# A graph network's edge weights: computed by TensorE in each layer from stored attributes, instead of stored and loaded

## The chip, the cores and the metric

The kernel runs on one core of a Trainium2 chip. The metric is the device time of one execution in microseconds (us), lower is better. A core has five engines that work through queues of their own and wait for each other by semaphores: PE (TensorE, matrix products into PSUM, with weight loads shown apart as PEld), DVE (VectorE), ACT (ScalarE), POOL (GpSimd) and SP (SyncE, which here only issues DMAs). Tiles lie in SBUF or in PSUM, and DRAM is reached by DMA.

## The reference

Three layers of a graph network with three relations, on N = 6250 nodes of D = 256 features and E = 100000 edges with 32 attributes each, then a residual and a layer norm:

```python
ew = edge_attr @ edge_w + edge_b
inv_cnt = [1.0 / jnp.maximum(jax.ops.segment_sum(m, dst, num_segments=n), 1.0) for m in rel_masks]
for l in range(N_LAYERS):
    residual = x
    msg = jax.nn.relu(x[src] * ew)
    out = jnp.zeros((n, D), dtype=x.dtype)
    for i in range(NUM_REL):
        h = jax.ops.segment_sum(msg * rel_masks[i][:, None], dst, num_segments=n)
        h = h * inv_cnt[i][:, None]
        out = out + h @ weights[l, i]
    out = out + x @ roots[l] + biases[l]
    x = residual + jax.nn.relu(out)
```

and at the end `_layernorm(x0 + x)`. The edge weights `ew` (E x 256) are the same in all layers. All is in float32. The edges come sorted by destination, and `dst` grows with the square of the edge's place, so that low nodes have many edges and high nodes few.

## The kernel before

A short first part looks at the edge lists and chooses a path; these inputs take `ordered_path`. Its unit is a *pair* of edge tiles, 2 x 128 edges; there are U = 391 pairs, and 49 node tiles of 128 nodes. One Python loop per layer, over `it`, writes out the order of every engine's queue by hand (a manual schedule), with each stage of a pair at a fixed distance from `it`:

- `gather` (L571 to L577, POOL), for the pair 8 steps ahead (AHEAD): two indirect DMAs fetch the 128 + 128 source rows of x into a tile xs (16 buffers).
- `weigh` (L612, DVE), 3 steps ahead: xs times the edge weights, in place; `bound` (L615, ACT): ReLU.
- `one_hot` (L619, DVE), 3 steps ahead: a 0/1 matrix per tile, 3 relations x 40 nodes (WIN) wide; its bfloat16 copy oh_b (L623, ACT) in layer 0 alone.
- `reduce` (L629, PE), at `it`: the products of messages and one-hots, 128 features x 120 columns, into a PSUM tile h_p. In layer 0 it counts edges too.
- `add` (L645, DVE), LAG steps behind: h_p is added to the accumulator acc in SBUF at a place read from the edge list. LAG is 1 in layer 0 and 3 in layers 1 and 2, with 2 and 5 buffers of h_p.
- Node tiles, when their edges are done (`starts`): `node_mul` (L673, PE, 12 products), `node_end` (L704 and L705, DVE), the store of the new rows to x_mid in DRAM (L707, SP), `clear` of acc (L690, ACT). The root term of each node tile (L650, L654, L658, L661) is made earlier, spread over the layer. The last layer adds the norm.

A layer's gathers read what the layer before stored in x_mid, all of it, so each layer starts when the last node tile of the one before is stored. `schedule` (L818) turns the pairs' order so that the first K = 60 pairs come last.

The edge weights before: in layer 0 only, `load_attrs` (L527, SP) loads attributes, `turn` (L589, PE) transposes two pairs of them, `keep_attrs` (L595, ACT) copies them to SBUF, `make_ew` (L602, PE) makes four products of 33 attribute rows (32 and a one for the bias) with edge_w into the PSUM tile ew_p (one buffer[...]), and `keep_ew` (L609, ACT) copies that into ew_s in SBUF. `store_ew` (L581, SP) keeps ew_s in DRAM as ew_all, 256 KB a pair. In layers 1 and 2 `load_ew` (L552, SP) loads it again, four pairs at a time. `weigh` reads ew_s in every layer.

Of the kernel before, what the change touches and what calls it, by code (L numbers as in the profile page):

```python
# [8 lines left out]
F32 = mybir.dt.float32  # L9
BF = mybir.dt.bfloat16  # L10
I32 = mybir.dt.int32
AF = mybir.ActivationFunctionType
ALU = mybir.AluOpType
AX = mybir.AxisListType
PSUM = bass.MemoryType.PSUM
# [13 lines left out]
def general_path(  # L29
# [24 lines left out]
    NP = NT * P  # L54
    K = R * NP
    HI = K // P
# [386 lines left out]
def ordered_path(ctx, tc, x, edge_attr, weights, roots, biases, edge_w, edge_b, out, src_i, seg, place_i, consts):  # L443
# [4 lines left out]
    nc = tc.nc  # L448
    P = 128
    N, D = x.shape  # L450
# [5 lines left out]
    U = T // 2  # L456
    A1 = A + 1
    DC = D // P
    UP = P // 2
    AR = UP + A1  # L460
    WK = R * WIN
    AHEAD = 8
    order, _, moved, least, most = schedule(N, E, 1)
    reach = []
    for u, (lo, hi) in enumerate(zip(least, most)):
# [7 lines left out]

    dram = ctx.enter_context(tc.tile_pool(name="dram_o", bufs=1, space=DRAM))

    ew_all = dram.tile([(U + 3) // 4, P, 8 * D], F32, name="ew_all")
    x_mid = [dram.tile([N, D], F32, name=f"x_mid{l}") for l in range(L - 1)]

    big = ctx.enter_context(tc.tile_pool(name="big", bufs=1))
# [27 lines left out]
    edge = ctx.enter_context(tc.tile_pool(name="edge", bufs=2))  # L507
# [1 line left out]
    o_pool = ctx.enter_context(tc.tile_pool(name="o_p", bufs=1, space=PSUM))  # L509
    r_pool = ctx.enter_context(tc.tile_pool(name="r_p", bufs=1, space=PSUM))  # L510


    groups = list(dict.fromkeys(u // 4 for u in order))

    def first_of(p, n):
        return p == 0 or order[p - 1] // n != order[p] // n

    def last_of(p, n):
        return p == U - 1 or order[p + 1] // n != order[p] // n
# [25 lines left out]
        nc.sync.dma_start(b_sb, biases[l:l + 1, :].to_broadcast([P, D]))  # L545
        return r_sb, b_sb

    def load_ew(l, g):
        ew = edge.tile([P, 4, 2, D], F32, name="ew_s", bufs=3)
        if l > 0:  # L550
            n = min(4, U - 4 * g)
            nc.sync.dma_start(ew[:, :n].rearrange("p k i d -> p (k i d)"), ew_all[g, :, :n * 2 * D])  # L552
        return ew

    def layer(l, r_sb, b_sb, ews, pools):
        h_pool = pools.enter_context(tc.tile_pool(name="h_p", bufs=2 if l == 0 else 5, space=PSUM))
        if l == 0:
            ew_pool = pools.enter_context(tc.tile_pool(name="ew_p", bufs=1, space=PSUM))
            t_pool = pools.enter_context(tc.tile_pool(name="turn_p", bufs=1, space=PSUM))

        LAG = 1 if l == 0 else 3
        starts = schedule(N, E, LAG)[1]
        moved = schedule(N, E, LAG)[2]
        x_rows = x if l == 0 else x_mid[l - 1]
        w_sb = wpool.tile([P, R * DC, D], F32, name="w_sb")
        CH = DC + 1 if l == 0 else DC
        xs, ew_ps, ats, ohs, h_ps, turns, o_ps, rs = {}, {}, {}, {}, {}, {}, {}, {}
        x0s, mvs, oh_bs, t_ss, places = {}, {}, {}, {}, []
        r_next, ews_next = (None, None), {}

        def gather(u):  # L571
            xs[u] = edge.tile([P, 2, D], F32, name="xs", bufs=16)
# [3 lines left out]
                    out=xs[u][:, i, :], out_offset=None, in_=x_rows[:, :],  # L576
                    in_offset=bass.IndirectOffsetOnAxis(ap=src_i[:, t:t + 1], axis=0))  # L577

        def store_ew(g):
            n = min(4, U - 4 * g)  # L580
            nc.sync.dma_start(ew_all[g, :, :n * 2 * D], ews[g][:, :n].rearrange("p k i d -> p (k i d)"))  # L581

        def pairs_of(q):
            return range(min(2, U - 2 * q))
# [6 lines left out]

        def keep_attrs(q):
            n = len(pairs_of(q))
            ats[q] = edge.tile([AR, 2, P], F32, name="at", bufs=1)
            nc.scalar.activation(ats[q][:, :n], turns[q][:AR, :n, :], AF.Copy)  # L595

        def make_ew(q):

            ew_ps[q] = ew_pool.tile([P, 2, 2, D], F32, name="ew_p")
            for k in pairs_of(q):  # L600
                for i in range(2):
                    nc.tensor.matmul(ew_ps[q][:, i, k, :], ats[q][i * UP:i * UP + A1, k, :],  # L602
                                     ew_sb[i * UP:i * UP + A1, :], start=True, stop=True)

        def keep_ew(q):
            if q // 2 not in ews:
                ews[q // 2] = load_ew(0, q // 2)
            for k in pairs_of(q):
                nc.scalar.activation(ews[q // 2][:, q % 2 * 2 + k], ew_ps[q][:, :, k, :], AF.Copy)  # L609

        def weigh(u):
            nc.vector.tensor_mul(xs[u], ews[u // 4][:, u % 4], xs[u])  # L612

        def bound(u):
            nc.scalar.activation(xs[u], xs[u], AF.Relu)  # L615
# [125 lines left out]
        for it in range(-9, max(starts) + 6):  # L741
            def pair(k):
                return order[it + k] if 0 <= it + k < U else None
            if pair(AHEAD) is not None:
                gather(pair(AHEAD))
            if l == 0 and pair(9) is not None and first_of(it + 9, 4):
                load_attrs(pair(9) // 4)
            if l > 0 and pair(AHEAD) is not None and pair(AHEAD) // 4 not in ews:
                ews[pair(AHEAD) // 4] = load_ew(l, pair(AHEAD) // 4)
            if l == 0 and it >= -4 and (it + 4) % 20 == 0 and (it + 4) // 20 * 6 < NT - 1:  # L750
                load_x((it + 4) // 20 * 6)
            if it == 10:
                nc.sync.dma_start(w_sb, weights[l].rearrange("r (c p) e -> p (r c) e", p=P))
            if l == L - 1 and it + 2 in root_at:
                load_x0(root_at[it + 2])
            if l < L - 1 and it == U - 10:
                r_next = load_root(l + 1)
            if l < L - 1 and U <= it < U + 2:
                ews_next[groups[it - U]] = load_ew(l + 1, groups[it - U])

            if pair(0) is not None:
                reduce(pair(0))
            if pair(3) is not None:
                weigh(pair(3))
                bound(pair(3))
            if pair(-LAG) is not None:
                add(pair(-LAG))
            if l == 0:

                for k, work in ((4, keep_ew), (5, make_ew), (6, keep_attrs), (7, turn)):  # L770
                    if pair(k) is not None and first_of(it + k, 2):
                        work(pair(k) // 2)
                if pair(3) is not None and last_of(it + 3, 4):
                    store_ew(pair(3) // 4)
            if it in root_at:
                root_turn(root_at[it])
            if it - 1 in root_at:
                root_turned(root_at[it - 1])
            if it - 2 in root_at:
                root_mul(root_at[it - 2])  # L780
            if it - 4 in root_at:
                root_keep(root_at[it - 4])
            if it == moved:
                move()
            if it - 2 == moved:
                clear(P)
            if it + 1 in node_at and slot_of(node_at[it + 1]) == 0:
                wrap()
            if it in node_at:
                node_mul(node_at[it], 0)  # L790
            if it - 1 in node_at:
                node_mul(node_at[it - 1], 1)
            if it - 3 in node_at:
                node_end(node_at[it - 3])
                clear(slot_of(node_at[it - 3]))
            if it - 4 in node_at and l == L - 1:
                norm(node_at[it - 4])
            if pair(3) is not None:
                one_hot(pair(3))
        return (*r_next, ews_next)  # L800

    with tc.manual_schedule():
        state = (*load_root(0), {})
# [4 lines left out]

WIN = 40
RING = 1024
ASIDE = RING + WIN
ROOTS = 16
PACK = 2048


def schedule(N, E, lag):  # L818

    P = 128
    U = -(-E // (2 * P))
    NT = -(-N // P)
    done = []
    for c in range(NT):
        edges = E * min(1.0, (P * (c + 1) / N) ** 0.5)
        done.append(U if c == NT - 1 else min(U, -(-int(edges) // (2 * P)) + 4))  # L830
    K = -(-done[0] // 4) * 4
    order = list(range(K, U)) + list(range(K - 1, -1, -1))
    moved = done[1] - K + lag
    starts = [0] * NT
    step = moved
    for c in range(2, NT):
        step = starts[c] = max(done[c] - K + lag + 1, step + 4)

    whole = U - int(0.55 * K)
    starts[1] = max(whole + lag, step + 4)  # L840
    starts[0] = max(U + lag - 1, starts[1] + 4)

    node = lambda e: int(N * min(1.0, max(0.0, e / E)) ** 2)
    least = [node(2 * P * u - 1024) for u in range(U)]
    most = [node(2 * P * u + 1024) for u in range(U)]


    for p, u in enumerate(order, lag):
        if u >= K:
            assert all(p <= starts[c] or least[u] >= P * (c + 1) for c in range(2, NT))  # L850
            assert p <= moved or least[u] >= 2 * P
            assert all(p < starts[c] or least[u] >= P * c for c in range(8, NT, 8))
            for b in range(RING // P + 1, (most[u] + WIN - 1) // P + 1):
                assert (moved + 2 if b - RING // P == 1 else starts[b - RING // P] + 3) < p
        else:
            assert most[u] <= 2 * P and (p <= starts[1] or most[u] + WIN <= P)
    return order, starts, moved, least, most
# [149 lines left out]
```

## Time and profile before

| | before |
|---|---|
| median of 3 runs | 3129.4 us (3127.76 to 3131.86) |
| profiled execution | 3133.5 us |
| its span, first to last instruction | 3131.7 us |
| granted PE clock, mean | 0.855 |
| first gather of layers 0, 1, 2 starts at | 38.3, 1082.1, 2104.1 us |
| last gather of layers 0, 1, 2 starts at | 1064.9, 2086.5, 3111.4 us |
| DMA packets | 668.14 MB, mean 213 GB/s |

The profile is one execution, taken on the chip. Its page has each engine's busy time and share of the span, and rows of digits for 40 equal slices of it (tenths of busy time; for PEclk tenths of the full TensorE clock that was granted). A group's row reads: line, engine, operation, out<-in, shape and count, busy time, mean ns of one, then the idle time of the engine just before and what ended most of it. "issue" is idle time in which the engine waited for nothing that the profile shows. [...] Some answers of the trace are finer: who waited for whom, busy times by stretches of time, and instructions in order of time.

### The profile page before, as it was taken

What the parts mean: (1) busy time and instruction counts of PE and PEld (TensorE: products, weight loads), DVE (VectorE), ACT (ScalarE), POOL (GpSimd) and SP (SyncE); (2) the same over time, 40 slices, a digit from 0 to 9 for tenths busy, and PEclk for the clock granted to TensorE, in tenths of its full rate; (3) what the DMA queues carried; (4) which work ended last, traced back from release to release, by engine and by line L of the source; (5) the groups of instructions that cost most, each with busy time, mean ns of one, the idle gap of its engine ahead of it and who ended that gap; (6) DMA issues with size and microseconds to landing.
All of it is one profiled execution on the core that took longest, in us unless ns stands there. A gap on an engine that the chain in (4) does not pass through costs nothing.

```text
span 3131.7 us, 50860 instructions
## 1 busy us (share of the span) xinstructions
PE 2429.6 (78%) x14938; PEld 2108.6 (67%) x14938; DVE 2003.2 (64%) x4664; ACT 1302.0 (42%) x2524; POOL 2354.9 (75%) x3118
## 2 busy tenths in 40 slices
PE   4898999999998766677777777767677777877765
PEld 3777777778887666666666666656566666666665
DVE  4566666777776455566666666645566677777765
ACT  3666666666776422222333333222223333333332
POOL 7777777777777677777777777767777777777775
PEclk9899899999998778778888888766887888888886
DMA  4777776766776665656666666656666666666664
GB/s 135 233 233 231 222 241 213 228 216 217 230 231 213 217 218 199 213 200 218 205 217 205 221 221 217 206 184 223 211 208 223 220 217 209 224 228 216 218 216 138
DMA packets 295322, 668.14 MB, mean 213 GB/s; under 512 B 147224, under 2 KB 181996, under 8 KB 257788
## 3 DMA queue, kind: packets, MB, share of 16 engines
q1 hardware_dynamic: 175832, 350.27, 32.2%
q0 software_dynamic: 112608, 307.65, 31.6%
q10 hardware_dynamic: 6596, 6.87, 0.6%
q8 instruction: 124, 2.03, 0.3%
q14 instruction: 162, 1.33, 0.1%
HBM read 542.90 MB, written 121.70 MB: 212 GB/s over the span
## 4 chain that ended last, share of the span: by engine, by line
PE 31%; DMA 21%; issue 19%; POOL 17%; DVE 9%; ACT 2%; DVEq 1%; POOLq 0%; ACTq 0%
POOL xs L575 16%; PE h_p L629 15%; DMA xs<-x_mid,src_io 15%; PE o_p L673 7%; DMA xs<-in_x_dram,src_io 6%; PE ew_p L602 4%; DVE x_root L704 3%; DVE xs L612 2%; PE r_p L658 2%; DVE acc L645 2%; PE turn_p L589 1%; ACT ew_s L609 1%; POOL limits L926 1%; DVEq L645 1%; DVE oh L619 1%
## 5 line engine op out<-in xcount | busy, mean ns | idle before, releaser
L575 POOL DMA_INDIRECT xs<-x_mid,src_io x1564 | 1537.5, 983 | 509.0 <-issue 404.6
L629 PE MATMUL h_p<-oh,xs 128*128 128x120 f32 x9384 | 1451.6, 311 | 445.0 <-issue 177.8
L629 PEld LDWEIGHTS h_p<-oh,xs 128*128 128x128 f32 x9384 | 1364.3, 223 | 541.6 <-issue 309.4
L612 DVE TENSOR_TENSOR xs<-ew_s,xs 128x512 f32<-128x512 f32 x1173 | 808.0, 689 | 913.5 <-DMA xs<-x_mid,src_io 566.8
L615 ACT ACTIVATE xs<-xs 128x512 f32<-128x512 f32 x1173 | 739.5, 630 | 1484.9 <-DVE xs L612 1466.3
L575 POOL DMA_INDIRECT xs<-in_x_dram,src_io x782 | 789.6, 1010 | 247.1 <-issue 158.7
L645 DVE TENSOR_TENSOR acc<-h_p,acc 128x240 f32 (+1 forms) x1173 | 519.5, 443 | 147.0 <-PE h_p L629 74.7
L673 PE MATMUL o_p<-w_sb,acc 128*128 128x256 f32 (+1 forms) x1764 | 503.5, 428 | 89.2 <-DVE acc L645 52.1
L619 DVE TENSOR_TENSOR oh<-iota_w,seg_o 128x240 f32<-128x240 f32 x1173 | 467.0, 398 | 0.0
L673 PEld LDWEIGHTS o_p<-w_sb,acc 128*128 128x128 f32 (+1 forms) x1764 | 361.7, 216 | 152.4 <-DVE acc L645 57.6
L658 PE MATMUL r_p<-r_sb,t_s 128*128 128x256 f32 x588 | 216.3, 504 | 79.5 <-ACT t_s L654 78.8
L602 PE MATMUL ew_p<-ew_sb,at 33*128 33x256 f32 x1564 | 235.2, 421 | 10.9 <-ACT at L595 8.8
L609 ACT ACTIVATE ew_s<-ew_p 128x512 f32<-128x512 f32 x391 | 209.4, 587 | 41.5 <-PE ew_p L602 40.5
L704 DVE SCALAR_TENSOR_TENSOR x_root<-o_p,inv,x_root 128x256 f32<-128x256 f32 (+1 forms) x441 | 212.4, 482 | 20.9 <-PE o_p L673 8.6
L623 ACT ACTIVATE oh_b<-oh 128x240 bf16<-128x240 f32 x391 | 160.0, 409 | 117.9 <-DVE oh L619 111.0
L658 PEld LDWEIGHTS r_p<-r_sb,t_s 128*128 128x128 f32 x588 | 130.0, 245 | 111.3 <-ACT t_s L654 95.5
L602 PEld LDWEIGHTS ew_p<-ew_sb,at 33*128 33x128 f32 x1564 | 141.7, 195 | 44.8 <-ACT at L595 16.3
L690 ACT ACTIVATE acc<-zero_o 128x768 f32<-128x768 f32 (+1 forms) x150 | 141.0, 940 | 15.8 <-PE o_p L673 9.2
L629 PE MATMUL h_p<-oh_b,full_ones 128*128 128x120 bf16 x782 | 109.3, 223 | 0.0
L589 PE MATMUL turn_p<-ident_o,an 128*128 128x128 f32 x391 | 89.4, 312 | 7.9 <-DMA an<-in_edge_attr_dram 7.8
L589 PEld LDWEIGHTS turn_p<-ident_o,an 128*128 128x128 f32 x391 | 40.7, 145 | 77.1 <-issue 75.9
L650 PE MATMUL r_p<-ident_o,x_all 128*128 128x128 f32 x294 | 64.1, 303 | 30.9 <-DVE x_root L661 24.8
(84 smaller groups left out, 609.0 us busy)
## 6 DMA issues: line engine op xcount, KB each, us to landing
ew_s<-ew_all SPq DMA_DIRECT2D x194, 1024.0 KB
ew_all<-ew_s SPq DMA_DIRECT2D x97, 1024.0 KB
xs<-x_mid,src_io POOLq DMA_INDIRECT x1564
xs<-in_x_dram,src_io POOLq DMA_INDIRECT x782
an<-in_edge_attr_dram SPq DMA_DIRECT2D x97, 128.0 KB
x_mid<-x_all SPq DMA_DIRECT2D x96, 128.0 KB
x_all<-in_x_dram ACTq DMA_DIRECT2D x8, 768.0 KB
x<-in_x_dram SPq DMA_DIRECT2D x48, 128.0 KB
```

Of the source, the lines that this page charges most:

```text
L575: nc.gpsimd.indirect_dma_start(out=xs[u][:, i, :], out_offset=None, in_=x_rows[:, :], in_offset=bass.IndirectOffsetOnAxis(ap=src_i[:, t:t ...
L589: nc.tensor.transpose(turns[q][:, k, :], ans[groups.index(q // 2) % 3][:, q % 2 * 2 + k].rearrange("p i a -> p (i a)"), ident)
L602: nc.tensor.matmul(ew_ps[q][:, i, k, :], ats[q][i * UP:i * UP + A1, k, :], ew_sb[i * UP:i * UP + A1, :], start=True, stop=True)
L609: nc.scalar.activation(ews[q // 2][:, q % 2 * 2 + k], ew_ps[q][:, :, k, :], AF.Copy)
L612: nc.vector.tensor_mul(xs[u], ews[u // 4][:, u % 4], xs[u])
L615: nc.scalar.activation(xs[u], xs[u], AF.Relu)
L619: nc.vector.tensor_tensor(ohs[u], iota_w[:, None, :].to_broadcast([P, 2, WK]), seg[:, 2 * u:2 * u + 2, None].to_broadcast([P, 2, WK]), op= ...
L629: nc.tensor.matmul(h_ps[u][:, d, :], xs[u][:, i, d * P:(d + 1) * P] if d < DC else full_ones, (ohs if d < DC else oh_bs)[u][:, i, :], star ...
L645: nc.vector.tensor_tensor(there, h_ps[u][:, :CH].rearrange("p c (r w) -> p c r w", r=R), there, op=ALU.add)
L658: nc.tensor.matmul(rs[c][:, 1, :], t_ss[c][:, d, :], r_sb[:, d, :], start=(d == 0), stop=(d == DC - 1))
L673: nc.tensor.matmul(o_p[:n, r, :], acc[:, d, r, slot:slot + n], w_sb[:, r * DC + d, :], start=(d == 0), stop=(d == DC - 1))
L704: nc.vector.scalar_tensor_tensor(root, o_p[:n, r, :], inv[:n, c, r:r + 1], root, op0=ALU.mult, op1=ALU.add)
```

## The change

The weights are no longer kept. ew_p, the PSUM tile that `make_ew` writes, is now made in every layer, and `weigh` reads it there; `keep_ew`, ew_s, `store_ew` and `load_ew` go. What is kept in DRAM is the transposed attributes, 64 KB a pair: `keep_attrs` writes them into a tile of 8 pairs (GROUP), `store_at` stores it in layer 0, `load_at` loads it in layers 1 and 2. `make_ew` for two pairs now stands ahead of `reduce` on PE, 3 steps before their use; the two weighs stand together, behind `add`. `turn` and `keep_attrs` come a step or more closer. [...]

```diff
-    AHEAD = 8
+    AHEAD = 9
...
-    ew_all = dram.tile([(U + 3) // 4, P, 8 * D], F32, name="ew_all")
+    at_all = dram.tile([(U + GROUP - 1) // GROUP, P, GROUP * P], F32, name="at_all")
...
-    def load_ew(l, g):
-        ew = edge.tile([P, 4, 2, D], F32, name="ew_s", bufs=3)
+    def load_at(l, g):
+        at = edge.tile([P, GROUP, P], F32, name="at", bufs=3)
         if l > 0:
-            n = min(4, U - 4 * g)
-            nc.sync.dma_start(ew[:, :n].rearrange("p k i d -> p (k i d)"), ew_all[g, :, :n * 2 * D])
-        return ew
-
-    def layer(l, r_sb, b_sb, ews, pools):
-        h_pool = pools.enter_context(tc.tile_pool(name="h_p", bufs=2 if l == 0 else 5, space=PSUM))
+            nc.sync.dma_start(at[:, :pairs_in(g)].rearrange("p k e -> p (k e)"), at_all[g, :, :pairs_in(g) * P])
+        return at
+
+    def layer(l, r_sb, b_sb, ats, pools):
+        h_pool = pools.enter_context(tc.tile_pool(name="h_p", bufs=2 if l == 0 else 3, space=PSUM))
+        ew_pool = pools.enter_context(tc.tile_pool(name="ew_p", bufs=1, space=PSUM))
         if l == 0:
-            ew_pool = pools.enter_context(tc.tile_pool(name="ew_p", bufs=1, space=PSUM))
...
-        LAG = 1 if l == 0 else 3
+        LAG = 1 if l == 0 else 2
...
-            ats[q] = edge.tile([AR, 2, P], F32, name="at", bufs=1)
-            nc.scalar.activation(ats[q][:, :n], turns[q][:AR, :n, :], AF.Copy)
+            g = 2 * q // GROUP
+            if g not in ats:
+                ats[g] = load_at(0, g)
+            nc.scalar.activation(ats[g][:, 2 * q % GROUP:2 * q % GROUP + n], turns[q][:, :n, :], AF.Copy)
...
-                    nc.tensor.matmul(ew_ps[q][:, i, k, :], ats[q][i * UP:i * UP + A1, k, :],
+                    nc.tensor.matmul(ew_ps[q][:, i, k, :],
+                                     ats[2 * q // GROUP][i * UP:i * UP + A1, (2 * q + k) % GROUP, :],
                                      ew_sb[i * UP:i * UP + A1, :], start=True, stop=True)
 
-        def keep_ew(q):
-            if q // 2 not in ews:
-                ews[q // 2] = load_ew(0, q // 2)
-            for k in pairs_of(q):
-                nc.scalar.activation(ews[q // 2][:, q % 2 * 2 + k], ew_ps[q][:, :, k, :], AF.Copy)
-
         def weigh(u):
-            nc.vector.tensor_mul(xs[u], ews[u // 4][:, u % 4], xs[u])
+            nc.vector.tensor_mul(xs[u], ew_ps[u // 2][:, :, u % 2, :], xs[u])
...
+            two = [order[p] for p in range(it + 3, min(it + 5, U)) if order[p] // 2 == pair(3) // 2] if (
+                pair(3) is not None and first_of(it + 3, 2)) else []
+            if two:
+                make_ew(two[0] // 2)
             if pair(0) is not None:
                 reduce(pair(0))
-            if pair(3) is not None:
-                weigh(pair(3))
-                bound(pair(3))
             if pair(-LAG) is not None:
                 add(pair(-LAG))
+            for u in two:
+                weigh(u)
+                bound(u)
             if l == 0:
 
-                for k, work in ((4, keep_ew), (5, make_ew), (6, keep_attrs), (7, turn)):
+                for k, work in ((5, keep_attrs), (6, turn)):
                     if pair(k) is not None and first_of(it + k, 2):
                         work(pair(k) // 2)
-                if pair(3) is not None and last_of(it + 3, 4):
-                    store_ew(pair(3) // 4)
+                if pair(3) is not None and last_of(it + 3, GROUP):
+                    store_at(pair(3) // GROUP)
...
-    K = -(-done[0] // 4) * 4
+    K = -(-done[0] // GROUP) * GROUP
```

More of the change, by code (lines that the diff above doesn't have):

```diff
@@ L459, in ordered_path @@
     UP = P // 2
-    AR = UP + A1
     WK = R * WIN
-    AHEAD = 8
+    AHEAD = 9
     order, _, moved, least, most = schedule(N, E, 1)
@@ L513, in ordered_path @@
     groups = list(dict.fromkeys(u // 4 for u in order))
+    at_groups = list(dict.fromkeys(u // GROUP for u in order))
     def first_of(p, n):
@@ L546, in load_root, with pairs_in @@
         return r_sb, b_sb
-    def load_ew(l, g):
-        ew = edge.tile([P, 4, 2, D], F32, name="ew_s", bufs=3)
+    def pairs_in(g):
+        return min(GROUP, U - GROUP * g)
+    def load_at(l, g):
+        at = edge.tile([P, GROUP, P], F32, name="at", bufs=3)
         if l > 0:
-            n = min(4, U - 4 * g)
-            nc.sync.dma_start(ew[:, :n].rearrange("p k i d -> p (k i d)"), ew_all[g, :, :n * 2 * D])
-        return ew
-    def layer(l, r_sb, b_sb, ews, pools):
-        h_pool = pools.enter_context(tc.tile_pool(name="h_p", bufs=2 if l == 0 else 5, space=PSUM))
+            nc.sync.dma_start(at[:, :pairs_in(g)].rearrange("p k e -> p (k e)"), at_all[g, :, :pairs_in(g) * P])
[3 more added lines that the diff above has]
+        ew_pool = pools.enter_context(tc.tile_pool(name="ew_p", bufs=1, space=PSUM))
         if l == 0:
-            ew_pool = pools.enter_context(tc.tile_pool(name="ew_p", bufs=1, space=PSUM))
             t_pool = pools.enter_context(tc.tile_pool(name="turn_p", bufs=1, space=PSUM))
-        LAG = 1 if l == 0 else 3
+        LAG = 1 if l == 0 else 2
         starts = schedule(N, E, LAG)[1]
@@ L566, in layer @@
         CH = DC + 1 if l == 0 else DC
-        xs, ew_ps, ats, ohs, h_ps, turns, o_ps, rs = {}, {}, {}, {}, {}, {}, {}, {}
+        xs, ew_ps, ohs, h_ps, turns, o_ps, rs = {}, {}, {}, {}, {}, {}, {}
         x0s, mvs, oh_bs, t_ss, places = {}, {}, {}, {}, []
-        r_next, ews_next = (None, None), {}
+        r_next, ats_next = (None, None), {}
         def gather(u):
@@ L577, in gather, with store_at @@
                     in_offset=bass.IndirectOffsetOnAxis(ap=src_i[:, t:t + 1], axis=0))
-        def store_ew(g):
-            n = min(4, U - 4 * g)
-            nc.sync.dma_start(ew_all[g, :, :n * 2 * D], ews[g][:, :n].rearrange("p k i d -> p (k i d)"))
+        def store_at(g):
+            nc.sync.dma_start(at_all[g, :, :pairs_in(g) * P], ats[g][:, :pairs_in(g)].rearrange("p k e -> p (k e)"))
         def pairs_of(q):
@@ L747, in layer @@
                 load_attrs(pair(9) // 4)
-            if l > 0 and pair(AHEAD) is not None and pair(AHEAD) // 4 not in ews:
-                ews[pair(AHEAD) // 4] = load_ew(l, pair(AHEAD) // 4)
+            if l > 0 and pair(AHEAD) is not None and pair(AHEAD) // GROUP not in ats:
+                ats[pair(AHEAD) // GROUP] = load_at(l, pair(AHEAD) // GROUP)
             if l == 0 and it >= -4 and (it + 4) % 20 == 0 and (it + 4) // 20 * 6 < NT - 1:
@@ L758, in layer @@
             if l < L - 1 and U <= it < U + 2:
-                ews_next[groups[it - U]] = load_ew(l + 1, groups[it - U])
+                ats_next[at_groups[it - U]] = load_at(l + 1, at_groups[it - U])
+            two = [order[p] for p in range(it + 3, min(it + 5, U)) if order[p] // 2 == pair(3) // 2] if (
+                pair(3) is not None and first_of(it + 3, 2)) else []
+            if two:
+                make_ew(two[0] // 2)
             if pair(0) is not None:
                 reduce(pair(0))
-            if pair(3) is not None:
-                weigh(pair(3))
-                bound(pair(3))
             if pair(-LAG) is not None:
                 add(pair(-LAG))
+            for u in two:
+                weigh(u)
+                bound(u)
             if l == 0:
-                for k, work in ((4, keep_ew), (5, make_ew), (6, keep_attrs), (7, turn)):
+                for k, work in ((5, keep_attrs), (6, turn)):
                     if pair(k) is not None and first_of(it + k, 2):
                         work(pair(k) // 2)
-                if pair(3) is not None and last_of(it + 3, 4):
-                    store_ew(pair(3) // 4)
+                if pair(3) is not None and last_of(it + 3, GROUP):
+                    store_at(pair(3) // GROUP)
             if it in root_at:
@@ L799, in layer @@
                 one_hot(pair(3))
-        return (*r_next, ews_next)
+        return (*r_next, ats_next)
     with tc.manual_schedule():
@@ L814 @@
 ROOTS = 16
+GROUP = 8
 PACK = 2048
```

## The prediction

> **What bounds the kernel now.** I first read the page for the engines' shares, then who waits for whom on POOL, then the gathers' own rows, and last the order of time around a long gather. The page alone does not settle it: four engines are busy.
>
> ```profile
> PE 2429.6 (78%) x14938; PEld 2108.6 (67%) x14938; DVE 2003.2 (64%) x4664; ACT 1302.0 (42%) x2524; POOL 2354.9 (75%) x3118
> PEclk9899899999998778778888888766887888888886
> DMA  4777776766776665656666666656666666666664
> L612 DVE TENSOR_TENSOR xs<-ew_s,xs 128x512 f32<-128x512 f32 x1173 | 808.0, 689 | 913.5 <-DMA xs<-x_mid,src_io 566.8
> L602 PE MATMUL ew_p<-ew_sb,at 33*128 33x256 f32 x1564 | 235.2, 421 | 10.9 <-ACT at L595 8.8
> ```
>
> POOL is busy for only 75%, but its waits (engine and line, ended by: us in total, times, longest) show what the other 25% are:
>
> ```profile
> POOL xs L575 <- issue: 563.3, 1848, 0.6
> POOL xs L575 <- PE h_p L629: 40.8, 134, 0.3
> POOL xs L575 <- DMA x_mid<-x_all: 32.8, 2, 16.6
> ```
>
> No wait is longer than 0.6 us, but for the two layer boundaries. 563.3 us over 1848 waits is 0.305 us, the same before every gather whatever is put down as its cause: it is the price of starting a gather. The gathers' durations (ns: least, median, most):
>
> ```profile
> L575 POOL DMA_INDIRECT xs<-x_mid,src_io x1564: 942/946/1456, 1082.1 to 3111.4; - x196
> L575 POOL DMA_INDIRECT xs<-in_x_dram,src_io x782: 942/946/1627, 38.3 to 1064.9; - x196
> ```
>
> So POOL runs without a break from 38.3 us to the end. Two gathers of 0.946 + 0.305 us make 2.50 us a pair of edge tiles, and 2346 of them make 2935 us. The rest: 38.3 us ahead, 16.0 and 16.4 us extra at the boundaries (17.2 and 17.7 us from the last gather's start to the next layer's first, less the 1.25 that is counted), 19.0 us behind the last, and the time by which gathers exceed 946 ns. That is (983 - 946) x 1564 + (1010 - 946) x 782 = 107.9 us by the means of the page's groups. The sum is 3132; the span is 3131.7.
>
> What stretches a gather is seen in the order of time (start, duration, engine, line):
>
> ```profile
> 1054.20 0.69 DVE L612 TENSOR_TENSOR xs<-ew_s,xs 128x512 f32<-128x512 f32 x1 [5.33 <-DMA xs<-in_x_dram,src_io]
> 1054.36 1.35 POOL L575 DMA_INDIRECT xs<-in_x_dram,src_io  x1 [0.30 <-issue]
> ```
> ```profile
> 1660.58 0.41 DVE L645 TENSOR_TENSOR acc<-h_p,acc 128x240 f32 x1 [1.70 <-PE o_p L673]
> 1660.64 0.95 POOL L575 DMA_INDIRECT xs<-x_mid,src_io  x1 [0.30 <-PE o_p L673]
> ```
>
> A gather that starts inside `weigh` (L612, both inputs in SBUF) takes 1.35 us; one that starts inside `add` (L645, one input in PSUM) takes its 0.95. I sorted all 2346 gathers by the DVE instruction in flight at their start. Those inside L612: 176, 163 and 141 in the three layers, stretched by 37.1, 23.4 and 22.0 us, together **82.4 us**. Inside the one-hots (L619, two SBUF inputs): 22.6 us. L705, L684, L687 and L499: some 3. Inside L645, L704 and L661, whose input is in PSUM: 557 gathers, none stretched (mean -0.6 ns). With no DVE instruction in flight: 873, none. A stretch is about what is left of the DVE instruction less 0.14 us.
>
> **The change, part by part.**
>
> *`weigh` reads PSUM.* Its operands become of L645's kind. The 82.4 us of stretch go; what is late next is the gather itself, at 2.50 us a pair. [...] The rows above decide: 480 gathers inside L612 are stretched by 172 ns on average, 557 inside PSUM readers by none. I take 82.4.
>
> Is `weigh` itself slower from PSUM? [...] The trace has a pair of one shape: L661 from PSUM 413 ns, L663 from SBUF 414. [...]
>
> *The one-hots stay.* Which gathers they meet depends on how DVE falls against POOL. Bounds: no overlap, -22.6 us; every one-hot met at its start, 1173 x (0.398 - 0.14) = 303, so +280. At random phase 0.258 x 0.258 / 2 / 1.27 us x 391 = 10 us a layer, 30 in all, against 22.6 now. I take +5.
>
> *`make_ew` in layers 1 and 2.* Eight matrix instructions for two pairs take 1.13 us at a granted clock of 1 (700.58 us in the order of time) and 2.08 at the low clock (1059.59): 0.57 to 1.04 us a pair on PE. PE's load in stages, by the windows (us of the window, busy time and count by engine, granted clock):
>
> ```profile
> 40.00:1065.00 1025.00, 943.78 (x6809) 788.26 (x6810) 685.71 (x1509) 682.46 (x1465) 787.30 (x781) 0.94 0.72 226
> 1082.00:2086.00 1004.00, 719.12 (x3966) 641.12 (x3966) 603.98 (x1406) 295.72 (x492) 766.24 (x781) 0.81 0.63 212
> 2104.00:3111.00 1007.00, 728.54 (x3969) 648.15 (x3970) 673.39 (x1651) 306.74 (x542) 768.93 (x781) 0.81 0.64 215
> ```
>
> Layer 1: 719.1 / 391 = 1.84 us a pair at clock 0.81, an estimated 1.49 at full clock. Plus 0.57 is 2.06. Layer 0 carries 943.8 x 0.94 / 391 = 2.27 in 2.62 us. The clock rises with the load: 0.81 at 72% busy, 0.94 at 92%, and 1.00 from 750 to 900 us, where PE is 98% busy. At an expected 0.90, the new load is 2.29 us of POOL's 2.50; at an unchanged 0.81, 2.54, about level with the gathers. [...] By the rows the low clock goes with an underloaded PE, and a PE that falls behind stops waiting; I take 0.90. So the work lies beside the gathers.
>
> *The new waits.* ew_p has one buffer. On PE `make_ew` waits for both weighs of the two pairs before, and behind it stand `reduce`, root and node work; DVE's `weigh` waits for `make_ew`, with `add` now ahead of it and one-hots and node ends behind. The loop costs 1.13 to 2.08 us on PE and 2 x 0.69 on DVE, under 3.5 of the 5.0 us that four gathers take. POOL is reached only through the 16 xs buffers: a gather needs the `reduce` 16 pairs back, 40 us, while `reduce` now starts 3 to 17 us after its gather ends. Some 23 us of PE delay cost nothing; beyond that all of it.
>
> *Layer 0* loses the copies L609 (209.4 us of ACT, 70 us of waits of DVE) and keeps its PE work. From 750 to 950 us PE is 97.9% busy at 2.58 us a pair, so it needs about 2.5 there: level with the new pace for 80 pairs. The cover of 23 us holds a shortfall up to 0.29 us a pair. I take 0; if the cover is gone, 10 to 20 us.
>
> *DMAs.* Weights moved: 391 pairs x 256 KB x 3 = 307 MB of the 668; attributes: 77 MB. 98 stores become 49 of 512 KB and 196 loads 98, on SP's queue, past the x_mid stores; buffers are free some ten steps early, so I see no new wait on SP. POOL waits for no landing, so the lighter traffic is worth nothing; before, DVE's 722 us of waits for landings are those of an engine that is ahead.
>
> *Ends of layers.* h_p has 3 buffers instead of 5 and LAG is 2 instead of 3, so after the last landing up to three reduces (1.05 to 2.06 us each) and six adds, not seven, remain. Between -2 and +3 us each for three ends; I take +1, so +3. K, AHEAD and moved nodes change no count of gathers, nor their order on POOL: nothing.
>
> **Sum.** 3131.7 - 82.4 + 5 + 3 = 3057.3 of span. The profiled execution was 3133.5 us with its span of 3131.7; the median of the runs is 3129.4, 2.3 under that span. So 3129.4 - 74.4 = **3055.0**.
>
> **The rivals.**
>
> 1. *PE becomes the bound in layers 1 and 2 (slower, 0.11).* Place: `make_ew` on PE behind the weighs of the two pairs before. It decides once PE needs more than 2.57 + 37/782 = 2.62 us a pair there, which is a clock below 2.06/2.62 = 0.79. At 0.75: 2.75 us x 782 = 2148 against 2011 now; with layer 0's 37 us gained the time is about 3230. For it: clock 0.64 to 0.72 at each layer's start. Against it: no window has PE over 90% busy at a clock below 0.88.
> 2. *The stretch stays (within 0.2%, 0.05).* Gathers are held by `weigh` as before, or meet one-hots instead: about 3130. [...] Against it: 557 unstretched gathers.
> 3. *All stretch goes (0.09).* Two weighs in a row leave the one-hots between gathers: -107.9 + 3, so 3025.
> 4. *Layer 0 becomes PE-bound in its node stage (0.10):* 10 to 40 us over the forecast, 3065 to 3095, still faster.
>
> **How the numbers follow.** Main case 0.65 at 3055, by its own terms 3035 to 3080 (one-hots -15 to +15, ends -6 to +9). With rivals 3 and 4 faster has 0.84; within 0.2% (6 us, about what a measurement of this kernel can tell from no change) 0.05; slower 0.11. The range takes in rivals 3 and 4 and leaves out 1 and 2: 3025 to 3100.
>
> **What would show it.** Right: gathers keep a median of 946 ns and gaps of 0.305, the mean falls to some 960, none that starts in `weigh` is stretched; `weigh` stays near 689 ns; PE is 85 to 95% busy in layers 1 and 2 at a clock near 0.9; POOL still waits for nothing but boundaries. Wrong: waits of POOL for PE's h_p longer than 0.4 us, PE busy near 100% at a clock below 0.8 with long waits for DVE xs, gathers stretched inside `weigh`, or a one-hot share well over 40 us.

## The result and the profile after

The changed kernel took 3097.8 us (median of 4 runs, 3093.3 to 3100.4) against 3128.7 before: a ratio of 0.989, 95% interval 0.988 to 0.991. In a second set it was 3099.3 against 3132.8, 0.989 (0.988 to 0.991). It is faster by 31 to 34 us, some 1%, where 74 were forecast. The time lies in the stated range, near its upper end; the size of the gain was wrong.

The page after, of the lines that were read before:

```profile
PE 2712.3 (88%) x18066; PEld 2215.3 (72%) x18066; DVE 1993.6 (64%) x4664; ACT 1103.5 (36%) x2133; POOL 2282.6 (74%) x3118
PEclk9999999999999988899999999978888899999998
DMA  3555555554455544444444444434454454444443
L609 DVE TENSOR_TENSOR xs<-ew_p,xs 128x512 f32<-128x512 f32 x1173 | 767.4, 685 | 872.7 <-PE ew_p L604 613.0
L604 PE MATMUL ew_p<-ew_sb,at 33*128 33x256 f32 x4692 | 708.7, 422 | 89.5 <-DVE xs L609 69.7
```

Weighing is L609 now and takes 685 ns from PSUM, 689 before from SBUF. PE has three times the products into ew_p, and a higher clock (0.93 on average, 0.855 before). What DVE waits for most is no longer a landing but PE's products, 613 us in all. POOL's own waits and gathers:

```profile
POOL xs L576 <- issue: 524.1, 1708, 1.4
POOL xs L576 <- ACT xs L612: 67.4, 159, 4.3
POOL xs L576 <- DMA x_mid<-x_all: 20.2, 1, 20.2
```
```profile
L576 POOL DMA_INDIRECT xs<-x_mid,src_io x1564: 941/947/1474, 1072.8 to 3070.6; - x196
L576 POOL DMA_INDIRECT xs<-in_x_dram,src_io x782: 941/947/1272, 38.5 to 1051.7; - x196
```

The median gather is still 947 ns, but POOL has waits of up to 4.3 us, which it did not have. A gather that starts inside a weighing is no longer stretched:

```profile
698.52 1.29 DVE L609 TENSOR_TENSOR xs<-ew_p,xs 128x512 f32<-128x512 f32 x2 [0.77 <-PE ew_p L604]
698.78 0.95 POOL L576 DMA_INDIRECT xs<-in_x_dram,src_io  x1 [0.30 <-PE ew_p L604]
```

Sorting all 2346 gathers as in the prediction, and adding up POOL's idle time beyond 0.31 us a gather, accounts for the two profiled executions to within 1 us:

| us | before | after | difference |
|---|---|---|---|
| stretch of gathers that start in the weighing | 82.4 | 0.7 | -81.7 |
| stretch, one-hots | 22.6 | 25.7 | +3.1 |
| stretch, other | 2.8 | 9.0 | +6.2 |
| POOL's waits in layers 0, 1, 2 | 0, 0, 0 | 21.4, 0, 7.9 | +29.3 |
| last gather to the next layer's first or the end, three times | 17.2, 17.7, 20.3 | 21.1, 15.6, 20.9 | +2.4 |
| span | 3131.7 | 3091.5 | -40.2 |

So the gain came where it was forecast, and 29 us of it were given back as waits of POOL. They all lie in two stretches, 740 to 935 us and 2830 to 2955 us, late in layers 0 and 2, where node tiles end close together because high nodes have few edges (the *node stages*). In the stretches of layer 0 (us; busy time and count of PE, PEld, DVE, ACT, POOL; clock, DMA) POOL's count falls from 48 gathers in 60 us to 39, while PE is idle for some 4 to 5 us of each. The clock is 1.00 while the waits build up and 0.94 only in the stretch that has them:

```profile
620.00:680.00 60.00, 55.72 (x403) 45.31 (x402) 40.62 (x94) 29.72 (x64) 45.68 (x48) 1.00 0.52 150
680.00:740.00 60.00, 55.99 (x410) 45.67 (x409) 39.69 (x91) 27.47 (x59) 45.67 (x48) 1.00 0.53 150
740.00:800.00 60.00, 54.48 (x368) 43.66 (x367) 37.61 (x88) 27.25 (x59) 37.34 (x39) 0.94 0.44 123
```

### The profile page after: what moved, and what is told of

The parts are those of the page before. It is cut to its first block, busy times and chain, and to the rows that moved or that the text cites. A ratio compares the mean times of both kernels' runs of the same rounds, so it can differ in the third digit from the quotient of the medians.

```text
span 3091.5 us, 56591 instructions
## 1 busy us (share of the span) xinstructions
PE 2712.3 (88%) x18066; PEld 2215.3 (72%) x18066; DVE 1993.6 (64%) x4664; ACT 1103.5 (36%) x2133; POOL 2282.6 (74%) x3118
## 3 DMA queue, kind: packets, MB, share of 16 engines
q1 hardware_dynamic: 154664, 119.64, 12.4%
## 4 chain that ended last, share of the span: by engine, by line
PE 55%; DVE 14%; issue 11%; DMA 9%; POOL 7%; ACT 3%; DVEq 1%; ACTq 0%; POOLq 0%; SPq 0%
PE h_p L626 20%; PE ew_p L604 15%; PE o_p L670 12%; DMA xs<-x_mid,src_io 7%; DVE xs L609 6%; POOL xs L576 6%; PE r_p L655 4%; DVE x_root L701 4%; DMA xs<-in_x_dram,src_io 2%; PE turn_p L589 2%; ACT xs L612 1%; DVE acc L642 1%; ACT at L597 1%; POOL limits L929 1%; DVEq L642 1%
## 5 line engine op out<-in xcount | busy, mean ns | idle before, releaser
L576 POOL DMA_INDIRECT xs<-x_mid,src_io x1564 | 1500.1, 959 | 518.8 <-issue 366.7
L626 PEld LDWEIGHTS h_p<-oh,xs 128*128 128x128 f32 x9384 | 1228.6, 205 | 343.4 <-issue 190.4
L626 PE MATMUL h_p<-oh,xs 128*128 128x120 f32 x9384 | 1365.8, 297 | 109.2 <-ACT mv L710 42.7
L609 DVE TENSOR_TENSOR xs<-ew_p,xs 128x512 f32<-128x512 f32 x1173 | 767.4, 685 | 872.7 <-PE ew_p L604 613.0
L576 POOL DMA_INDIRECT xs<-in_x_dram,src_io x782 | 754.6, 965 | 268.7 <-issue 157.4
L604 PE MATMUL ew_p<-ew_sb,at 33*128 33x256 f32 x4692 | 708.7, 422 | 89.5 <-DVE xs L609 69.7
L604 PEld LDWEIGHTS ew_p<-ew_sb,at 33*128 33x128 f32 x4692 | 431.9, 196 | 239.9 <-issue 158.7
L670 PE MATMUL o_p<-w_sb,acc 128*128 128x256 f32 (+1 forms) x1764 | 463.0, 402 | 29.1 <-DVE acc L642 15.9
L670 PEld LDWEIGHTS o_p<-w_sb,acc 128*128 128x128 f32 (+1 forms) x1764 | 338.5, 202 | 75.8 <-DVE acc L642 17.9
L589 PEld LDWEIGHTS turn_p<-ident_o,an 128*128 128x128 f32 x391 | 40.2, 143 | 81.3 <-ACT at L597 72.4
L626 PEld LDWEIGHTS <-full_ones 128*128 128x128 bf16 x782 | 81.5, 104 | 2.4
L597 ACT ACTIVATE at<-turn_p 128x256 f32<-128x256 f32 x196 | 71.7, 366 | 0.8 <-PE turn_p L589 0.8
```

Source lines behind the costliest of these rows:

```text
L576: nc.gpsimd.indirect_dma_start(out=xs[u][:, i, :], out_offset=None, in_=x_rows[:, :], in_offset=bass.IndirectOffsetOnAxis(ap=src_i[:, t:t ...
L589: nc.tensor.transpose(turns[q][:, k, :], ans[groups.index(q // 2) % 3][:, q % 2 * 2 + k].rearrange("p i a -> p (i a)"), ident)
L604: nc.tensor.matmul(ew_ps[q][:, i, k, :], ats[2 * q // GROUP][i * UP:i * UP + A1, (2 * q + k) % GROUP, :], ew_sb[i * UP:i * UP + A1, :], st ...
L609: nc.vector.tensor_mul(xs[u], ew_ps[u // 2][:, :, u % 2, :], xs[u])
L626: nc.tensor.matmul(h_ps[u][:, d, :], xs[u][:, i, d * P:(d + 1) * P] if d < DC else full_ones, (ohs if d < DC else oh_bs)[u][:, i, :], star ...
L670: nc.tensor.matmul(o_p[:n, r, :], acc[:, d, r, slot:slot + n], w_sb[:, r * DC + d, :], start=(d == 0), stop=(d == DC - 1))
```

## The theories

*Order theory.* In the node stages PE and DVE wait for each other. The products into ew_p stand behind a node tile's work on PE, so DVE stands still before `weigh`; DVE's node end then comes after that, and behind it stand the `add`s that free h_p for PE's next `reduce`. Neither engine is full in the rows above. In layer 0 PE's transposes wait for ACT as well. The order of time in layer 2 shows one turn of it (PE makes its products from 2772.61 on and is then idle for 2.02 us, until DVE's `add` at 2775.27 has freed a buffer; the releaser that is named, ACT's L710, has nothing to do with h_p):

```profile
2770.54 1.29 DVE L609 TENSOR_TENSOR xs<-ew_p,xs 128x512 f32<-128x512 f32 x2 [2.21 <-PE ew_p L604]
2772.41 1.51 DVE L701 SCALAR_TENSOR_TENSOR x_root<-o_p,inv,x_root 128x256 f32<-128x256 f32 x3
2772.61 1.13 PE L604 MATMUL ew_p<-ew_sb,at 33*128 33x256 f32 x8
...
2775.27 0.40 DVE L642 TENSOR_TENSOR acc<-h_p,acc 128x240 f32 x1
...
2775.77 1.66 PE L626 MATMUL h_p<-oh,xs 128*128 128x120 f32 x8 [2.02 <-ACT mv L710]
```

*Capacity theory* (rival 4 of the prediction). PE has too much work in the node stage, and the same work in another order takes as long.

*Port and traffic theories*, on the gain: it is the stretch of gathers that start while DVE reads two SBUF inputs, 82.4 us in the weighing before and 0.7 after ("port" is only the theory's name: what holds such a gather no run shows); or it is the smaller DMA traffic, 438 MB for 668.

## The experiments

**A first set ran on another chip**, on which the kernel before took 3680.9 us and POOL waited for 660 to 714 us inside the layers in the three profiles; the times there say nothing of the 30 us in question. What they show is the stretch. On that chip all three forms were slower than the kernel before, by 5.3, 2.0 and 3.2%; the changed kernel as it stands was not run there. A fourth, the kernel before with a constant tile in place of the loads (x3), gave no time.

x1: ACT copies ew_p to SBUF, and the weighing reads the copy.

```diff
+        def keep_ew(u):
+            ew_ss[u] = edge.tile([P, 2, D], F32, name="ew_s", bufs=4)
+            nc.scalar.activation(ew_ss[u], ew_ps[u // 2][:, :, u % 2, :], AF.Copy)
         def weigh(u):
-            nc.vector.tensor_mul(xs[u], ew_ps[u // 2][:, :, u % 2, :], xs[u])
+            nc.vector.tensor_mul(xs[u], ew_ss[u], xs[u])
...
+            for u in two:
+                keep_ew(u)
             for u in two:
                 weigh(u)
```

> The changed kernel, but ACT copies ew_p into an SBUF tile and the weighing reads that, so its two inputs lie in SBUF again; DRAM traffic stays that of the changed kernel. Port theory (what the change gained is the stretch of gathers that start while DVE reads two SBUF inputs): gathers that start inside the weighing are stretched again by 60 to 90 us in all, and the time returns to 3125 to 3165. Traffic theory (the gain is the smaller DMA traffic, 438 MB for 668): the time stays at 3090 to 3105 and the gathers' mean near 960 ns.

Measured there: 3877.8 us, 98.2 us of stretch in the weighing, somewhat over the 60 to 90 expected. The port theory's sign and size; the time is not usable.

x2: the products earlier on PE, and in layer 0 the transposes and their copy a step earlier.

```diff
-            if two:
-                make_ew(two[0] // 2)
             if pair(0) is not None:
                 reduce(pair(0))
+            if pair(4) is not None and first_of(it + 4, 2):
+                make_ew(pair(4) // 2)
...
-                for k, work in ((5, keep_attrs), (6, turn)):
+                for k, work in ((6, keep_attrs), (7, turn)):
```

> The changed kernel with the same instructions, but the products into ew_p stand behind the reduce of the step before, ahead of that step's root and node work, and in layer 0 the transposes and their copy are one step earlier. Order theory (POOL's 30 us of waits in the node stages come from PE and DVE waiting for each other: the weighing stands still until the products behind a node's work are made, and reduce until the adds behind the weighing are): the waits of POOL beyond 0.31 us fall to under 12 us and the time to 3070 to 3085. Capacity theory (PE lacks time in layer 0's node stage, rival 4): PE has the same work, so 3093 to 3103.

Measured there: 3760.0 us, no stretch in the weighing, 660 us of waits inside the layers. Inconclusive on the order.

x4: without the norm.

```diff
-            nc.vector.bn_stats(stats[:n], x_all[:n, c, :])
...
-            nc.vector.bn_aggr(mv[:n, :nc.vector.BN_AGGR_DIM], stats[:n])
-            nc.scalar.activation(mv[:n, 2:3], mv[:n, 1:2], AF.Sqrt, bias=eps[:n])
...
-            nc.vector.reciprocal(mv[:n, 1:2], mv[:n, 2:3])
-            nc.vector.tensor_scalar(x_all[:n, c, :], x_all[:n, c, :], mv[:n, 0:1], mv[:n, 1:2],
-                                    op0=ALU.subtract, op1=ALU.mult)
```

> The changed kernel without the layer norm of the last layer (its statistics, square root, reciprocal and scaling are left out; rows are stored unnormalised). It takes some 1.2 us of DVE and no PE work from each node tile of layer 2. Order theory: POOL's waits in layer 2 (8 us beyond the start price) and the late weighing there go, layer 0's 22 us stay; 8 to 12 us less than the changed kernel. Capacity theory: PE's work is unchanged in layer 2, so the waits there stay, 0 to 2 us less.

Measured there: 3801.9 us. Inconclusive. These three were run again elsewhere, with the changed kernel beside them.

**The second set** ran where the kernel before took 3132.8 us.

> The changed kernel itself, as the measure for the other runs of this chip. Expected: 3093 to 3101, if the chip runs the kernel before in about 3129; where the chip is slower throughout, only ratios to this run count.

Measured: 3099.3 us; POOL's waits 17.5, 0 and 10.3 us in the three layers.

> The changed kernel, but ACT copies ew_p into an SBUF tile and the weighing reads that, so its two inputs lie in SBUF again; traffic stays that of the changed kernel. Port theory: gathers that start inside the weighing are stretched again, by 60 to 90 us in all; 3125 to 3165. Traffic theory: 3090 to 3105.

Measured: **3284.8 us** (1.048, 1.046 to 1.050). The stretch in the weighing is back at 39.2, 29.1 and 42.0 us in the three layers, 110 in all and more than the 60 to 90 expected, as in this gather inside the pair of weighings that starts at 1599.98:

```profile
1599.98 1.29 DVE L613 TENSOR_TENSOR xs<-ew_s,xs 128x512 f32<-128x512 f32 x2 [1.36 <-ACT ew_s L610]
...
1600.68 1.41 POOL L576 DMA_INDIRECT xs<-x_mid,src_io  x1 [0.30 <-PE h_p L630]
```

The port theory stands on the stretch, not on the time, which is 120 us beyond its range: 116 us are waits of POOL in layers 0 and 2. More than half are put down to the copies (122.9 us, of which 195 starts at 0.305 us are 59):

```profile
POOL xs L576 <- ACT ew_s L610: 122.9, 195, 3.2
POOL xs L576 <- ACT xs L616: 29.3, 10, 6.8
```

A third engine between PE's products and the weighing makes the loop longer still; this fits the order theory, but does not test it.

> The changed kernel with the same instructions, but the products into ew_p stand behind the reduce of the step before, ahead of that step's root and node work, and in layer 0 transposes and copy one step earlier. Order theory: POOL's waits beyond the start price fall from 30 to under 12 us; 3070 to 3085. Capacity theory: PE has the same work, so the time of the changed kernel within 5 us.

Measured: **3067.1 us** (0.978, 0.977 to 0.980), 32 us less than the changed kernel beside it with the same instructions. POOL's waits are those of the boundaries:

```profile
POOL xs L576 <- issue: 522.8, 1715, 0.3
...
POOL xs L576 <- DMA x_mid<-x_all: 19.7, 1, 19.7
POOL xs L576 <- DMA x<-in_x_dram: 16.2, 1, 16.2
```

(The last is the boundary of layers 1 and 2, put down to another DMA.) Of the stage from 560 to 780 us the waits say why. The changed kernel (its first profile), then x2b:

```profile
DVE xs L609 <- PE ew_p L604: 42.3, 26, 3.7
...
PE turn_p L589 <- ACT at L597: 7.6, 10, 0.9
```
```profile
DVE xs L609 <- PE ew_p L604: 6.8, 14, 0.5
```

And in the stretch where the changed kernel's POOL fell to 39 gathers, x2b has 47 with PE 98% busy:

```profile
740.00:800.00 60.00, 59.03 (x441) 49.55 (x438) 43.95 (x102) 31.14 (x65) 45.77 (x47) 1.00 0.53 152
```

Capacity falls as the cause of the waits: the same work is done in time. It is close, though. The time from a gather's end to its `reduce` measures how far PE is behind, and between pairs 180 and 270 of layer 0 it grows from 15.9 to 39.5 us in the changed kernel, but also from 12.4 to 22.3 in x2b. So some 10 of the 24 us are there without the bad order, with PE 94 to 98% busy, and the order adds the rest.

x3b: the kernel before without loads of weights in layers 1 and 2.

```diff
-        ew = edge.tile([P, 4, 2, D], F32, name="ew_s", bufs=3)
-        if l > 0:
-            n = min(4, U - 4 * g)
-            nc.sync.dma_start(ew[:, :n].rearrange("p k i d -> p (k i d)"), ew_all[g, :, :n * 2 * D])
-        return ew
+        return edge.tile([P, 4, 2, D], F32, name="ew_s", bufs=3) if l == 0 else None
...
-            nc.vector.tensor_mul(xs[u], ews[u // 4][:, u % 4], xs[u])
+            nc.vector.tensor_mul(xs[u], ews[u // 4][:, u % 4] if l == 0 else x_all[:, 40:42, :], xs[u])
```

> The kernel before without the loads of edge weights in layers 1 and 2; the weighing there takes two fixed rows' tiles of the node table in SBUF in their place, so the weights are left out of these layers. About 205 MB less traffic of 668. Port theory: POOL waits for no landing, so within 10 us of the kernel before (3120 to 3138). Traffic theory: at least the gain of the change, 3100 or less.

Measured: 3134.0 us, ratio 1.0007 (0.9996 to 1.0019). In layers 1 and 2 the core moves 109 and 116 GB/s instead of 212 and 215, and nothing is gained. The traffic theory falls.

**The third set** took the early order apart (the kernel before: 3130.4 us).

x5 has only the second of x2's two edits (`turn`, `keep_attrs`), x6 only the first (`make_ew`).

> The changed kernel with only the second half of the early order: in layer 0 the transposes and their copy stand one step earlier; the products into ew_p stay where the change put them. If the transposes' waits for ACT (some 50 us of PE before the transposes in the changed kernel) are what holds layer 0: its 20 us of POOL waits go, layer 2's 8 to 10 stay, 3076 to 3084. If the products' place is it: 3093 to 3101.

> The changed kernel with only the first half: the products into ew_p behind the reduce of the step before; transposes and copy stay. If the products' place is the cause in both layers: no waits of POOL beyond the start price, 3064 to 3072. If layer 0 hangs on the transposes: layer 2's 8 to 10 us go, layer 0's stay, 3084 to 3092.

> The changed kernel without the layer norm of the last layer (statistics, square root, reciprocal and scaling left out; rows are stored unnormalised). It takes 1.2 us of DVE and no PE work from each node tile of layer 2. Order theory (PE stands behind DVE's node work there): layer 2's 8 to 10 us of POOL waits go and layer 0's 17 to 21 stay; 3084 to 3092. If layer 2's waits come from PE's own load, they stay: 3094 to 3101.

x8 is the kernel before with the buffers and lag of the change.

```diff
-        h_pool = pools.enter_context(tc.tile_pool(name="h_p", bufs=2 if l == 0 else 5, space=PSUM))
+        h_pool = pools.enter_context(tc.tile_pool(name="h_p", bufs=2 if l == 0 else 3, space=PSUM))
...
-        LAG = 1 if l == 0 else 3
+        LAG = 1 if l == 0 else 2
```

> The kernel before with only LAG 2 and 3 buffers of h_p in layers 1 and 2. The prediction's sum gave this part -2 to +3 us at each of two layer ends and nothing elsewhere: 3125 to 3138. If fewer buffers alone hold POOL in the node stages: 3140 or more, with waits of POOL beyond the start price.

| | time, us | ratio to before, its interval | POOL's waits in layers 0, 1, 2, us | longest from a gather's end to its `reduce`, us |
|---|---|---|---|---|
| kernel before (first profile) | 3128.7 | 1 | 0, 0, 0 | 17.9, 15.6, 16.5 |
| changed kernel (second set) | 3099.3 | 0.989 (0.988 to 0.991) | 17.5, 0, 10.3 | 46.0, 16.9, 42.7 |
| x5, transposes earlier | 3073.3 | 0.983 (0.981 to 0.985) | 0.4, 0, 11.8 | 36.7, 17.2, 45.9 |
| x6, products earlier | 3072.6 | 0.981 (0.979 to 0.983) | 6.4, 0, 0 | 39.7, 14.9, 27.6 |
| x2b, both (second set) | 3067.1 | 0.978 (0.977 to 0.980) | 0, 0, 0 | 24.8, 14.9, 25.1 |
| x4b, no norm | 3083.9 | 0.986 (0.984 to 0.988) | 14.8, 0, 0 | 43.8, 16.1, 17.3 |
| x8, lag and buffers alone | 3129.6 | 1.000 (0.999 to 1.001) | 0, 0, 0 | 18.6, 15.6, 20.9 |

The last column shows the cover of the 16 xs buffers: POOL waits only where it passes some 37 us (the prediction had 40).

In layer 2, of the two edits only the products' place matters (x6 against x5). The node work counts there too: without the norm, with PE's work the same, the waits go (x4b), while layer 0's stay. The norm's steps are DVE's, but for a square root on ACT that waits for DVE, and x4b takes both away, so it doesn't say which of the two held PE. In layer 0 either edit takes most of the waits away, because either brings the longest distance down to about the cover. Neither expectation of x5 and x6 had this: both said that one of the two edits would do nothing in layer 0. The fewer buffers of h_p cost nothing by themselves (x8); what they do beside the products in layers 1 and 2 was not tried.

x5 gains 26 us on the changed kernel of the second set, which is more than the 17 us of layer 0. The two traces account for 22: 16 us fewer waits over all layers, 5 us less stretch and 1 us at the ends. The other 4 are scatter: the changed kernel's profiled execution was the fastest of its set, x5's was its median.

## Why the prediction was right and wrong

- *POOL is the bound, 0.946 + 0.305 us a gather:* right, in both first profiles outside the two stretches with waits; x2b has no other waits from start to end than the boundaries.
- *82.4 us of stretch go:* right, 81.7, and 110 came back with SBUF inputs (x1b). 480 gathers inside the weighing were stretched by 172 ns on average before, and 526 by 1 ns after. What of a gather is held, its read of the row numbers (src_io) or another part, no run here separates.
- *`weigh` no slower from PSUM:* right, 685 ns from PSUM and 689 from SBUF, means of 1173 each.
- *One-hots +5:* +3.1. Stretch by all other DVE operations, taken at nothing without a reason, +6.2, of which 4 in those with two SBUF inputs (L702, L660, L681 and L684).
- *PE at 2.29 us a pair and a clock of 0.90 in layers 1 and 2:* the window from 1080 to 2050 us has 849.1 us of PE for 769 gathers, 2.21 us a pair, at 0.92. Rival 1, PE as the bound at a clock below 0.79, did not come.
- *Traffic worth nothing:* right (x3b). *Ends of layers +3:* +2.4.
- *The new waits, and layer 0 at 0:* **this is the step that failed.** The sum was that "the loop costs 1.13 to 2.08 us on PE and 2 x 0.69 on DVE", and that a cover of 23 us holds a shortfall of 0.29 us a pair for 80 pairs. The loop was counted without what stands in it: node work ahead of the products on PE, node ends between the weighings and the next `add` on DVE, h_p's release behind both, and in layer 0 ACT's copy and the transposes, which the prediction named in the change and never costed. The cover itself was right. But PE falls behind by 0.26 us a pair from about pair 180 on (the 15.9 to 39.5 us above), at a clock of 1.00, and pair 180 is gathered at 495 us, 255 us before the 750 us from which the prediction counted its 80 pairs. With the early order, 0.11 us a pair of it are left (x2b); the other 0.15 were waiting and not work. So the cover was used up at 740 us: 17 to 21 us of waits in layer 0, which is rival 4's size, though for the most part by another cause, and 8 to 10 in layer 2, where the prediction saw nothing.
- *From span to median:* the span came out at 3091.5 for 3057.3, 34 us over, of which 29 are the waits and 6 the other stretch. The median came out 43 over. The other 9 are scatter of single executions: the profiled one was the slowest before and the fastest after.

The early order gives 3067.1 us, 12 over the forecast. Its span is 8 us over (3065.3 for 3057.3), and 7 of these are again the stretch by other operations; the ends came as forecast (+2.7 for +3). The remaining 4 us lie between span and median, and the kernel before was 3.4 us slower in that set too.

## What to carry to other kernels

When a copy between two engines is taken out, they are bound to each other's order: walk once through both queues with everything that stands between the two instructions, node ends and buffer releases too, and not only the two durations. An engine that issues gathers can be the bound at 75% busy, as POOL was here; look whether its gaps are all the same length (0.305 us here), and then at what stretches its instructions. An instruction that makes something for another engine may belong ahead of the long work of its own step: the same instructions, with the products moved, and in layer 0 the transposes and their copy, gained another 32 us here. Measure on more than one chip: on one, the same early order was 2% slower than the kernel before.

## What the runs showed of the hardware

- The gathers on POOL that start inside the weighing with two SBUF inputs end late: 480 in the kernel before, by 172 ns on average. Where more than 0.2 us of the weighing is left, they are late by that rest less 0.13 us in the median (1.35 us for 0.95 in the kernel before, 1.41 in x1b). Inside DVE instructions with one input in PSUM they are late by nothing: 557 gathers before, -0.6 ns on average, and 526 inside the weighing after, 1 ns.
- One chip ran the kernel before in 3681 us and another in 3131. On the slower one a gather takes no longer, 959 and 962 ns on average in x2 against 959 and 965 in the changed kernel on a faster one; waits are longer (POOL's longest under "issue" 6.4 us in x2, 1.4 in the changed kernel), even inside the row of eight products of a `reduce` (13, 31 and 32 us in all in x1, x2 and x4, none in the kernel before and the changed kernel on the faster chips). The cause was not sought, and the kernel before has no profile there.
